# A two-layer network on one core: the last pair of heads by tiles, another rule for TensorE in the list planner, new due times, products of zeros

## The chip, the cores and the metric

The kernel runs on one core of a Trainium2 chip. The core has five engines with instruction queues of their own: PE (TensorE, the matmuls), DVE (VectorE), ACT (ScalarE), POOL (GpSimd) and SP (SyncE, which here only starts DMA transfers). Each engine works through its queue in order; waits between engines go through semaphores. The metric is the time of one execution on the device in microseconds, lower is better.

## The reference, cut to what matters

The input x has 4 sequences of 512 tokens with 512 features, in float32. Four blocks follow one another, each as x = x + layernorm(f(layernorm(x))).

```python
# 1: state space, 16 heads of 64 (1024 channels)
x = x + _layernorm(_L0_attn_ref(_layernorm(x), ...))
# 2: shared expert and 2 of 8 routed experts
x = x + _layernorm(_L0_ffn_ref(_layernorm(x), ...))
# 3: 16 heads of 128, a delta rule over time
def step(St, inp):
    q_, k_, v_, a_, b_ = inp
    sk = jnp.einsum('bhij,bhj->bhi', St, k_)
    err = sk - v_
    Sn = a_[..., None, None] * St - b_[..., None, None] * err[..., None] * k_[..., None, :]
    o_ = jnp.einsum('bhij,bhj->bhi', Sn, q_)
    return (Sn, o_)
...
o = (o - mu) * jax.lax.rsqrt(var + 1e-05) * ln_w + ln_b
g = jax.nn.sigmoid(x @ Wg).reshape(B, S, NH, D)
return (o * g).reshape(B, S, NH * D) @ Wo
# 4: 2 of 8 experts, chosen for a whole sequence
logits = x0 @ switch_w.T + switch_b
probs = jax.nn.softmax(logits, axis=-1)
gate, top_idx = jax.lax.top_k(probs, TOPK)
...
out = x + o
return out @ w3.T + b3
```

## The kernel before

Tokens are handled in tiles of 128 rows, four to a sequence (TPB). The program has three parts: `state_space` (block 1, up to some 430 us), `experts` (block 2, to some 900 us) and `upper_layer` (blocks 3 and 4, the rest).

**Opening.** SP first loads the first sequence's four tiles x[0] to x[3] (L266), then the identity matrix in `const` (L268), then in `state_space` the first half of w_in, the small parameters `prm`, half of w_gate, the other halves, the rest of `const`, and w_out (L380 to L386). POOL fills a tile `zero` (L395), which SP later writes over a buffer in memory (L474).

**Planned lists.** `state_space` and `upper_layer` don't issue their work directly. They describe it to a `Plan`: each `op` has an engine, a cost in us, a due time, the operations it comes after, and the buffers ("slots") it uses. `sequence` (L186) then simulates the engines by these costs: over and over, each engine's candidates are the operations whose predecessors are all placed, and the one that can start first is taken; among those that could start at the same time the earlier due time wins. `ahead` bounds how far past the earliest open due time an operation may be taken. The result is the fixed order of each engine's list; on the chip the semaphores decide when each instruction runs. For an operation of PE the model adds 0.2 us (`DRAIN`) before anything that comes after it may start, another PE operation included, and 0.1 us (`CROSS`) from engine to engine. A load in the model takes 0.42 us of SP and lands some 3.5 us later. Loads of x that start the first layer are a made-up engine "LD".

The due times are a sum of a sequence's or a pair's number and a parameter in `DUE` (L18). In the first layer the unit is a sequence: its norm is due at the number less `norm`, its projections at the number, the gate's at +`sigma`, the scans at +`scan`, the output products at +`out`. In the upper layer the unit is one of 32 pairs of heads (8 to a sequence).

**A sequence of the first layer** (`sequence(b, due)` within `state_space`): each x tile is loaded (L606), its mean and variance are taken on DVE (L434) and POOL, it is normalised into one of two `xn` buffers (L450), turned by four PE transposes (L618) and copied by ACT (L628). Projections (L462) take four products in one PSUM bank; ACT and three DVE instructions (L676) make a convolution of them, which frees the bank. The tag `mm` has four banks.

**A pair of heads**: `prepare` projects and convolves q, k, v, makes the masked score blocks and stores 32x32 blocks to memory; `solve` loads them back as `lb` (L1722), solves by rows on DVE (L1748, L1757), stores the result and loads it into `yi` (L1766, L1773); `merge` builds full inverses with small PE products and copies `xx`, `wt`, `w`, `yi` (L1795, L1807); `recur` goes through four chunks of 128 tokens in sequence; each chunk leaves a tile `o` for both heads and sums of squares `ss`. `finish` (L2028) waits for all chunks, computes 8 reciprocal roots at once on POOL, scales 8 pieces of `o` on ACT (L2071), turns four pieces per head (L2085), applies the norm's weights while moving to `oT` (L2092), multiplies the gate on POOL (L2106), and multiplies by `wo` for the four tiles (16 instructions), adding to `y` (L2148).

After a sequence's last pair `route` norms y, adds the row from memory (L2222), stores it back (L2231), norms it again in place (L1224, once the store has landed), turns it into `zT`, and computes the router's logits; DVE then chooses experts and mixes their weights. `experts_of` applies them (L2446, L2465) and ends with products by `w_o`, a norm, a sum (L2502) and the output's store (L2510). `begin` gathers the next sequence's rows and prepares its input.

The main loop at the end of `upper_layer` calls these for the 32 pairs.

Of the kernel before, what the change touches and what calls it, by code (L numbers as in the profile page):

```python
# [9 lines left out]
F32 = mybir.dt.float32  # L10
# [5 lines left out]
BANKS = {"mm": 4, "tr": 2, "sq": 2}  # L16

DUE = dict(  # L18
    half=0.13, last=0.17, out=1.7, norm=0.27, late=0.0, dt=0.28, sigma=0.66, scan=1.76, early=3.8,
    seam=0.18, head=0.5, qkv=0.1, score=0.0, keys=0.46, solve=0.83, rows=0.2, merge=1.73,  # L20
    recur=1.45, step=0.44, finish=2.42, gate=0.0, turn=0.07, sum=0.88, route=3.33, begin=0.77,
    spread=1.55, ahead=3.0, last_finish=2.86, last_route=2.65, last_spread=0.0, fetch=0.6,
    pick=0.03, experts=1.07, next=0.38, experts2=1.62, experts3=2.7, close3=0.36, tile=0.02,
    half_router=0.0, mix=0.68, close=0.15, closes=0.0,
)
ENGINES = [getattr(mybir.EngineType, n) for n in ("PE", "DVE", "Activation", "Pool", "SP")]

P = 128
# [80 lines left out]
class Plan:  # L109
# [59 lines left out]
    def sequence(self):  # L169
        for n, op in enumerate(self.ops):  # L170
            op.place = (op.due, n)
            op.missing = len(op.after)
            for o in op.after:
                o.then.append(op)
        waiting, clock, order = {}, {}, []
        self.held, table = {"DVE": 0.0, "POOL": 0.0}, None
        by_due = sorted(self.ops, key=lambda op: op.place)
        first = 0
        for op in self.ops:
            clock.setdefault(op.engine, 0.0)  # L180
            waiting.setdefault(op.engine, [])
            if not op.missing:
                waiting[op.engine].append(op)
        while len(order) < len(self.ops):
            while by_due[first].missing < 0:
                first += 1  # L186
            limit = by_due[first].due + self.ahead
            best = None
            for engine, ops in waiting.items():
                pick = None  # L190
                for op in ops:
                    if op.due > limit:
                        continue
                    at = self.start(op, clock[engine])
                    if at is not None and (pick is None or (at, op.place) < pick[:2]):
                        pick = (at, op.place, op)
                if pick and (best is None or pick[0] < best[0]):
                    best = pick
            assert best, "no operation can start"
            at, _, op = best  # L200
            waiting[op.engine].remove(op)
            for slot in op.slots:
                tag = self.tags[slot.tag]
                if slot not in tag["live"]:
# [46 lines left out]
def network(ctx: ExitStack, tc: tile.TileContext, a: dict, out: bass.AP):  # L251
# [6 lines left out]
    def ps(tag, shape=(P, 512)):  # L258
        return psum.tile(list(shape), F32, tag=tag, name=tag, bufs=BANKS[tag])
# [107 lines left out]
    def state_space():  # L367
        with (
# [768 lines left out]
    def upper_layer(first):  # L1137
        with (
# [41 lines left out]
            def row(shape=(P, D)):  # L1180
                return plan.slot(pl, "row", shape, ROWS, free=True)

            def lateslot(tag, shape, bufs):
                return plan.slot(plan.late, tag, shape, bufs)
# [840 lines left out]
                        )  # L2025
                return o, ss, outs, used

            def finish(seq, pair, o, ss, outs, y, due):  # L2028

                rs = lateslot("rso", [P, UNITS], 2)  # L2030

# [174 lines left out]
            def route(b, y, sums, due):  # L2206
# [2 lines left out]
                before = stored[b]  # L2209
                part = lateslot("part", [P, E2, KD], 1)  # L2210
                turned, prods, written = [], [], []
                for i in range(TPB):
# [26 lines left out]
                    turned.append(columns(zT, z, i, due + 0.1, [no]))  # L2239

# [279 lines left out]
            for n in range(B * NPAIR):  # L2520
                b, pair = divmod(n, NPAIR)
                if pair == 0:
# [12 lines left out]
                o, ss, outs, last = recur(heads, yi, inverse, n + DUE["recur"])  # L2535
                used[n] = [last, *inverse]
                sums = finish(
                    seq, pair, o, ss, outs, y, n + DUE["finish" if n < B * NPAIR - 1 else "last_finish"]
                )
                if pair == NPAIR - 1:  # L2540
                    routed.append(route(b, y, sums, n + DUE["route" if b < B - 1 else "last_route"]))
# [103 lines left out]
```

## Time and profile before

| | us |
|---|---|
| median of 3 runs | 2992.0 (2986.73 to 2998.78) |
| the profiled execution | 2973.44 |
| its span, first to last instruction | 2971.6 |
| PE busy | 2828.6 (95%) |
| DVE busy | 1831.5 (62%) |
| ACT busy | 1174.8 (40%) |
| POOL busy | 694.8 (23%) |
| mean granted clock of PE | 0.978 |

The span runs from the first to the last instruction; the profiled execution's time is 1.8 us longer than it. Busy shares are means over stages. The page also cuts the span into 40 slices of 74 us and gives each engine's busy share in tenths, 9 standing for 90% or more:

```profile
PE   8999999999998999899989899998999999999997
PEld 3444444455554456565645555554556655555553
DVE  4887532011114666776688776687786678867455
ACT  4653221111111355444544444453444544544530
POOL 1233403100004113321231422132231222221133
```

The first six slices are the first layer's state space, the next six its experts, and from the thirteenth on the pairs of heads follow. A timeline row has a start, a duration, the engine and line, the operation, output and input, the number of merged instructions, and in brackets how long the engine had been idle and what ended that.

### The profile page before, as it was taken

To read this page: it belongs to the slowest core of one execution; us is meant where nothing else is said; L and a number is where in the kernel's file an instruction comes from. 1 tells how busy PE (TensorE), PEld (TensorE's weight loads), DVE (VectorE), ACT (ScalarE), POOL (GpSimd) and SP (SyncE) were. 2 spreads that over 40 slices of the span, in tenths; PEclk is the share of its full clock that TensorE was granted. 3 is DMA by queue.
4 is the path that set the end of the run, shared out by engine and by line. 5 is a ranking of instruction groups with operands and counts; after the bars stand their busy time and mean duration, and the time that the engine had idled before them with its cause. 6 is when DMAs were issued, how large, how long until landed. Compare 5 with 4: busy or idle time off the path is not lost. (4 is left out here: it accounts for less than half of the span.)

```text
span 2971.6 us, 38915 instructions
## 1 busy us (share of the span) xinstructions
PE 2828.6 (95%) x13095; PEld 1579.5 (53%) x13095; DVE 1831.5 (62%) x4629; ACT 1174.8 (40%) x2423; POOL 694.8 (23%) x859
## 2 busy tenths in 40 slices
PE   8999999999998999899989899998999999999997
PEld 3444444455554456565645555554556655555553
DVE  4887532011114666776688776687786678867455
ACT  4653221111111355444544444453444544544530
POOL 1233403100004113321231422132231222221133
PEclk9999999999999999999999999998999999999999
DMA  5321213698983434433454433345432435533332
GB/s 190 95 87 41 89 46 129 220 320 316 318 280 108 124 77 104 123 83 85 100 140 144 134 89 92 84 129 158 123 116 70 97 98 139 140 82 81 100 128 89
DMA packets 289705, 383.99 MB, mean 129 GB/s; under 512 B 127490, under 2 KB 128130, under 8 KB 289250
## 3 DMA queue, kind: packets, MB, share of 16 engines
q1 hardware_dynamic: 275600, 347.51, 40.3%
q0 software_dynamic: 5120, 16.78, 1.6%
q10 hardware_dynamic: 8786, 17.22, 1.6%
q8 instruction: 104, 1.70, 0.2%
q14 instruction: 95, 0.78, 0.1%
HBM read 320.58 MB, written 60.82 MB: 128 GB/s over the span
## 5 line engine op out<-in xcount | busy, mean ns | idle before, releaser
L1199 PE MATMUL mm<-xT,wh 128*128 128x512 f32 x1536 | 739.1, 602 | 1.0 <-DVE cv L1590 1.0
L1590 DVE SCALAR_TENSOR_TENSOR cv<-mm,prm,cv 128x511 f32<-128x511 f32 (+2 forms) x576 | 427.2, 745 | 134.7 <-ACT cv L1579 124.8
L1199 PEld LDWEIGHTS mm<-xT,wh 128*128 128x128 f32 x1536 | 269.8, 192 | 218.4 <-issue 207.1
L1199 PE MATMUL mm<-wo,oT 128*128 128x512 f32 x512 | 271.4, 645 | 5.5 <-POOL oT L2106 1.8
L1748 DVE TENSOR_TENSOR term<-lb,xb 128x60 f32<-128x60 f32 (+24 forms) x992 | 213.2, 215 | 91.0 <-DMA lb<-blocks 75.5
L1199 PE MATMUL mm<-xT,wg 128*128 128x512 f32 x512 | 260.4, 596 | 0.1
L1757 DVE TENSOR_TENSOR xb<-xb,term 128x60 f32<-128x60 f32 (+24 forms) x992 | 226.7, 228 | 33.8
L1579 ACT ACTIVATE cv<-mm,prm 128x512 f32<-128x512 f32 x192 | 148.9, 776 | 192.5 <-PE mm L1199 189.3
L1672 POOL TENSOR_TENSOR kq<-qk,ag 128x384 f32<-128x384 f32 x128 | 119.3, 950 | 337.9 <-PE sq L1199 284.6
L1079 PE MATMUL mm<-gu,rT 128*128 128x352 f32 x624 | 190.9, 459 | 0.0
L1079 PEld LDWEIGHTS mm<-gu,rT 128*128 128x128 f32 x624 | 118.2, 190 | 76.1 <-issue 17.8
L1199 PE MATMUL sq<-S,kq 128*128 128x128 f32 x768 | 151.0, 279 | 6.8 <-DVE S L1963 6.8
L1199 PEld LDWEIGHTS sq<-S,kq 128*128 128x128 f32 x768 | 124.0, 193 | 44.0 <-issue 26.7
L1372 POOL DMA_INDIRECT got<-yg,index x32 | 37.6, 1174 | 446.1 <-DMA yg<-yo 365.7
L1199 PEld LDWEIGHTS mm<-wo,oT 128*128 128x128 f32 x512 | 94.0, 204 | 84.8 <-issue 67.9
L1605 ACT ACTIVATE qk<-cv 128x512 f32<-128x512 f32 x128 | 80.5, 629 | 136.6 <-DVE cv L1590 114.7
L1085 DVE TENSOR_TENSOR actr<-slr,mm 128x352 f32<-128x352 f32 x39 | 20.3, 521 | 183.1 <-PE mm L1079 178.6
L1199 PEld LDWEIGHTS sq<-const,vT 128*128 128x128 f32 x512 | 87.7, 192 | 80.2 <-issue 53.2
L462 PE MATMUL mm<-xT,w_in 128*128 128x512 f32 x256 | 123.2, 611 | 5.9 <-DVE cv L676 5.1
L1558 DVE TENSOR_TENSOR_SCAN m<-ag,m 128x516 f32<-128x516 f32 x64 | 95.7, 1499 | 52.2 <-DMA ag<-dd 38.2
L1199 PE MATMUL mm<-qk 128*128 128x256 f32 x512 | 123.7, 383 | 0.7 <-ACT qk L1605 0.7
L462 PE MATMUL mm<-xT,w_gate 128*128 128x512 f32 x256 | 123.3, 594 | 0.0
(302 smaller groups left out, 4778.2 us busy)
## 6 DMA issues: line engine op xcount, KB each, us to landing
gu<-in_gu SPq DMA_DIRECT2D x78, 704.0 KB
wh<-in_wh SPq DMA_DIRECT2D x192, 256.0 KB
ag<-dd SPq DMA_DIRECT2D x64, 516.0 KB
sw<-in_sw SPq DMA_DIRECT2D x96, 256.0 KB
dn<-in_dn SPq DMA_DIRECT2D x39, 512.0 KB
lb<-blocks SPq DMA_DIRECT2D x128, 128.0 KB
wg<-in_wg SPq DMA_DIRECT2D x64, 256.0 KB
wo<-in_wo SPq DMA_DIRECT2D x64, 256.0 KB
```

The source lines that it names most:

```text
L462: lambda: nc.tensor.matmul(p(), lhsT=lhsT(), rhs=rhs(), start=first, stop=last),
L1079: nc.tensor.matmul(dst, lhsT=rT[:, k, :], rhs=gu[:, k, lo : lo + F], start=k == 0, stop=k == KD - 1)
L1085: nc.vector.tensor_tensor(act, sl, pu, ALU.mult)
L1199: nc.tensor.matmul(dst, lhsT=lhsT, rhs=rhs, start=start, stop=stop)
L1372: nc.gpsimd.indirect_dma_start(out=to(), out_offset=None, in_=yg, in_offset=bass.IndirectOffsetOnAxis(ap=places[k][:, n : n + 1], axis=0), ...
L1558: nc.vector.tensor_tensor_scan(flat, ag()[:, 0, :], flat, 0.0, ALU.mult, ALU.add)
L1579: lambda p=p, cv=cv, j=j: nc.scalar.activation(cv(), p(), AF.Identity, bias=cb[:, j, h : h + 1], scale=cw[:, j, h, 3:4]),
L1590: lambda p=p, cv=cv, j=j, t=t: nc.vector.scalar_tensor_tensor(cv()[:, t:], p()[:, : S - t], cw[:, j, h, 3 - t : 4 - t], cv()[:, t:], ALU.mult,
L1605: lambda cv=cv, view=view: nc.scalar.activation(view(), cv(), AF.Silu),
L1672: lambda j=j: nc.gpsimd.tensor_tensor(kq()[:, j], chunk(qk()[:, j, :])[:, 1:, :], g()[:, 1:, j : j + P], ALU.mult,),
L1748: nc.vector.tensor_tensor(part(), lb()[:, i : i + 1, i + 1 :].to_broadcast([P, n, left]), xb()[:, :n, i : i + 1].to_broadcast([P, n, left] ...
L1757: nc.vector.tensor_tensor(rest, rest, part(), ALU.add)
```

## The change

It has these parts:

- In the planner, an operation of PE that comes after another one of PE may start when that one's cost is over; the 0.2 us of `DRAIN` are now added only towards other engines.
- 28 or so of the due parameters have other values, most of them in the first layer and in the last sequence's tail.
- `const`'s first part is loaded behind x[0] in place of x[3], and `prm` ahead of the weights.
- Six products of the zero tile into a bank of the tag `sq` stand at the head of PE's list.
- For the very last pair `finish` hands over to a new function `by_tile`: for each of the four tiles it scales, turns, moves, gates, multiplies by `wo` and adds to y, each tile coming after its own chunk's sums of squares.
- In `route` the second norm writes to y[i] instead of the row itself, so it no longer comes after the row's store; for the last sequence the tiles' due times step by `tile`.

```diff
@@ DUE
-    half=0.13, last=0.17, out=1.7, norm=0.27, late=0.0, dt=0.28, sigma=0.66, scan=1.76, early=3.8,
-    seam=0.18, head=0.5, qkv=0.1, score=0.0, keys=0.46, solve=0.83, rows=0.2, merge=1.73,
-    recur=1.45, step=0.44, finish=2.42, gate=0.0, turn=0.07, sum=0.88, route=3.33, begin=0.77,
-    spread=1.55, ahead=3.0, last_finish=2.86, last_route=2.65, last_spread=0.0, fetch=0.6,
-    pick=0.03, experts=1.07, next=0.38, experts2=1.62, experts3=2.7, close3=0.36, tile=0.02,
-    half_router=0.0, mix=0.68, close=0.15, closes=0.0,
+    half=0.12, last=0.43, out=2.02, norm=1.8, late=0.06, dt=0.0, sigma=0.87, scan=3.72, early=4.33,
+    seam=0.96, head=0.5, qkv=0.1, score=0.0, keys=0.46, solve=0.82, rows=0.29, merge=1.73,
+    recur=1.45, step=0.44, finish=2.42, gate=0.0, turn=0.07, sum=1.06, route=3.32, begin=0.98,
+    spread=1.55, ahead=3.0, last_finish=2.94, last_route=2.48, last_spread=0.27, fetch=0.53,
+    pick=0.46, experts=0.63, next=0.0, experts2=1.91, experts3=3.05, close3=0.17, tile=0.05,
+    half_router=0.0, mix=0.71, close=0.45, closes=0.0,
@@ Plan.sequence
             for o in op.then:
-                o.ready = max(o.ready, op.end + (self.CROSS if o.engine != op.engine else 0.0))
+                done = op.begin + op.us if o.engine == op.engine == "PE" else op.end
+                o.ready = max(o.ready, done + (self.CROSS if o.engine != op.engine else 0.0))
@@ network
+    const = glob.tile([P, CONST.shape[1]], F32, tag="const", name="const")
     for i in range(TPB):
         nc.sync.dma_start(x[i], x_in[i])
-    const = glob.tile([P, CONST.shape[1]], F32, tag="const", name="const")
-    nc.sync.dma_start(const[:, :P], a["const"][:, :P])
+        if i == 0:
+            nc.sync.dma_start(const[:, :P], a["const"][:, :P])
@@ state_space
+            nc.sync.dma_start(prm, a["p1"])
             for half in range(2):
...
-                    if w is w_in and not half:
-                        nc.sync.dma_start(prm, a["p1"])
...
+            idle = ps("sq")
+            for k in range(6):
+                nc.tensor.matmul(idle, lhsT=zero[:, :P], rhs=zero, start=True, stop=True)
...
-            for us, to in ((3.0, in_there), (0.6, None), (2.8, gate_there), (2.8, in_there), (2.8, gate_there)):
+            for us, to in ((0.6, None), (3.0, in_there), (2.8, gate_there), (2.8, in_there), (2.8, gate_there)):
@@ upper_layer
+            def by_tile(o, ss, rs, outs, gates, wos, y, due):
+                sums, oTs = [], [lateslot("oT", [P, S], 2) for _ in range(2)]
+                for i in range(TPB):
+                    d, two = due + DUE["tile"] * i, slice(2 * i, 2 * i + 2)
+                    def scale(two=two):
+                        rstd(rs()[:, two], ss()[:, two], EPS)
+                        nc.gpsimd.tensor_scalar(rs()[:, two], rs()[:, two], -(float(P) ** 0.5), None, ALU.mult)
+                    sc = op("POOL+", 1.2, d, scale, outs[two], [ss, rs])
...
+                    last = op("ACT", 0.6, d, scaled, [sc], [o[i], rs])
...
+                    last = op("PE", 0.35, d, turn, [last], [p, o[i], *oTs])
...
+                    last = op("ACT", 0.7, d, move, [last], [p, *oTs])
...
+                    last = op("POOL+", 0.75, d, gated, [last, *ready], [*oTs, *(g for g, _ in gates)])
+                    p = bank("mm")
+                    for j in range(2):
+                        wo, wl = wos[j]
+                        last = op("PE", 0.88, d, ..., [wl, last], [p, *oTs, wo, y[i]])
+                    sums.append(op("DVE", 0.7, d, ..., [last], [p, y[i]]))
+                return sums
...
-                sc = op("POOL+", 2.4, due, scale, outs, [ss, rs])
...
+                if last_pair:
+                    return by_tile(o, ss, rs, outs, gates, wos, y, due)
+                sc = op("POOL+", 2.4, due, scale, outs, [ss, rs])
@@ route
                 for i in range(TPB):
-                    xr = z = row()
+                    due = start + (DUE["tile"] * i if last else 0.0)
+                    xr, z = row(), y[i]
...
-                    no = normalised(z, xr, st, [xr], due, after=[written[i]])
+                    no = normalised(z, xr, st, [xr, z], due)
```

More of the change, by code (lines that the diff above doesn't have):

```diff
@@ L2026, in recur, with scaled, turn, move @@
                 return o, ss, outs, used
-            def finish(seq, pair, o, ss, outs, y, due):
+            def by_tile(o, ss, rs, outs, gates, wos, y, due):
[6 more added lines that the diff above has]
+                    sc = op("POOL+", 1.2, d, scale, outs[two], [ss, rs])
+                    def scaled(i=i):
+                        for j in range(2):
+                            nc.scalar.activation(
+                                o[i]()[:, j, :],
+                                o[i]()[:, j, :],
+                                AF.Copy,
+                                scale=rs()[:, 2 * i + j : 2 * i + j + 1],
+                            )
+                    last = op("ACT", 0.6, d, scaled, [sc], [o[i], rs])
+                    p = bank("tr")
+                    def turn(p=p, i=i):
+                        for j in range(2):
+                            nc.tensor.transpose(one(p(), j), o[i]()[:, j, :], ident)
+                    last = op("PE", 0.35, d, turn, [last], [p, o[i], *oTs])
+                    def move(p=p, i=i):
+                        for j in range(2):
+                            nc.scalar.activation(
+                                one(oTs[j](), i), one(p(), j), AF.Identity, bias=lnb, scale=lnw
+                            )
+                    last = op("ACT", 0.7, d, move, [last], [p, *oTs])
+                    def gated(i=i):
+                        for j in range(2):
+                            oT, gt = one(oTs[j](), i), one(gates[j][0](), i)
+                            nc.gpsimd.tensor_tensor(oT, oT, gt, ALU.mult)
+                    ready = [g for _, g in gates]
+                    last = op("POOL+", 0.75, d, gated, [last, *ready], [*oTs, *(g for g, _ in gates)])
+                    p = bank("mm")
+                    for j in range(2):
+                        wo, wl = wos[j]
+                        last = op(
+                            "PE",
+                            0.88,
+                            d,
+                            lambda i=i, j=j, p=p, wo=wo: mm(p(), one(oTs[j](), i), wo(), j == 0, j == 1),
+                            [wl, last],
+                            [p, *oTs, wo, y[i]],
+                        )
+                    sums.append(
+                        op(
+                            "DVE",
+                            0.7,
+                            d,
+                            lambda i=i, p=p: nc.vector.tensor_tensor(y[i](), y[i](), p(), ALU.add),
+                            [last],
+                            [p, y[i]],
+                        )
+                    )
+                return sums
@@ L2030, in finish @@
+            def finish(seq, pair, o, ss, outs, y, due, last_pair):
                 rs = lateslot("rso", [P, UNITS], 2)
@@ L2211, in route @@
                 turned, prods, written = [], [], []
+                last = b == B - 1
+                start = due
                 for i in range(TPB):
-                    xr = z = row()
+                    due = start + (DUE["tile"] * i if last else 0.0)
+                    xr, z = row(), y[i]
                     src = xs[b * TPB + i]
@@ L2237, in route @@
                     st = row_stats(xr, [xr], due, [ad])
-                    no = normalised(z, xr, st, [xr], due, after=[written[i]])
+                    no = normalised(z, xr, st, [xr, z], due)
                     turned.append(columns(zT, z, i, due + 0.1, [no]))
+                due = start
                 last = b == B - 1
@@ L2537, in upper_layer @@
                 sums = finish(
-                    seq, pair, o, ss, outs, y, n + DUE["finish" if n < B * NPAIR - 1 else "last_finish"]
+                    seq, pair, o, ss, outs, y, n + DUE["last_finish" if n == B * NPAIR - 1 else "finish"],
+                    n == B * NPAIR - 1,
                 )
```

## The prediction, made before the changed kernel was run

> **What bounds the kernel now.** I read the page's busy shares first, then PE's busy time by stage, PE's waits, the timeline of the first 45 us, that of the last 130 us, and last the stalls of the middle stage one by one. PE is busy 95% of the span, so only its idle time and its slow clock can be won.
>
> ```profile
> PE 2828.6 (95%) x13095; PEld 1579.5 (53%) x13095; DVE 1831.5 (62%) x4629; ACT 1174.8 (40%) x2423; POOL 694.8 (23%) x859
> ...
> 0.00:50.00 50.00, 36.62 (x85) 17.14 (x86) 21.81 (x40) 16.32 (x22) 6.64 (x20) 0.93 0.73 273
> 50.00:400.00 350.00, 349.58 (x912) 153.60 (x911) 248.48 (x455) 151.37 (x199) 112.76 (x112) 1.00 0.24 74
> ...
> 980.00:2800.00 1820.00, 1729.41 (x9708) 1035.58 (x9706) 1338.79 (x3670) 860.35 (x1916) 450.13 (x573) 0.97 0.42 109
> ...
> 2850.00:2900.00 50.00, 44.94 (x149) 24.98 (x150) 37.27 (x81) 8.62 (x14) 23.61 (x34) 0.97 0.44 153
> ...
> 2920.00:2940.00 20.00, 15.84 (x38) 5.67 (x38) 15.62 (x37) 3.81 (x5) 11.03 (x15) 0.95 0.31 105
> ```
>
> Each row gives a stretch, then PE's busy time first and the granted clock third from the end. PE idles 13.4 us in the first 50, 0.4 us in the rest of the first layer, 90.6 us in the 1820 us of the pairs of heads (where a mean clock of 0.97 costs another 45 to 64 us), and 5.1 and 4.2 us in two stretches of the tail. PE's waits name the causes:
>
> ```profile
> PE tr L1199 <- DVE xx L1795: 18.1, 9, 5.3
> PE tr L1199 <- ACT xx L1807: 15.6, 8, 5.9
> PE tr L1237 <- DVE row L1224: 13.0, 6, 6.3
> PE tr L1199 <- ACT w L1807: 11.8, 3, 5.4
> PE tr L1199 <- DVE kt L1701: 8.5, 4, 2.4
> PE tr L1199 <- issue: 7.6, 7, 3.4
> PE tr L618 <- DMA const<-in_const: 7.2, 1, 7.2
> ...
> PE mm L462 <- DVE cv L676: 5.1, 1, 5.1
> ```
>
> Total, times and longest wait follow each name. In 980 to 2800 there are 30 stalls of 0.8 us or more, 76.9 us together: 48.3 us in the merge of the inverses (xx, w and the unnamed ones), 28.6 us elsewhere. The worst merge stalls lie at the switches of sequences (1537 to 1670, 2009 to 2150, 2487 to 2613), where DVE waits up to 6 us for lb or yi to land.
>
> **Part A, the opening.** Removed: PE's first work waited for const at 7.17 although xn was there at 5.92; const now follows x[0]. Added: six products of zeros. A 128x512 f32 product is two instructions, 0.43 us each at full clock and 0.86 us at the opening's slow clock (weight loads follow at that distance from 13.20 to 15.76). With 4.2 us slow, as from 12.19 to 16.36, twelve take 5 x 0.86 + 7 x 0.43 = 7.3 us, from about 1.4 to 8.7; the third and fourth transposes wait for their norms (ending 9.3 and 10.3) anyway, so the projections would start near 11.6 instead of 12.19. Worth 0.6 us, and 2.1 us more if the clock then holds.
>
> The row on that: 16 transposes kept PE busy over 90% of 9.43 to 11.51 and the products behind them still ran at 0.86. The Trainium skill ("TensorE: Matmul & The Clock Gate", Part 4) says that transposes don't count as activity for the gate, and this row fits; by it the warmth would lapse again, and the 2.1 us be nothing.
>
> None of this reaches the end, because of the next wait:
>
> ```profile
> 12.19 9.91 PE L462 MATMUL mm<-xT,w_in 128*128 128x512 f32 x18 [0.67 <-ACT xT L628]
> ...
> 26.44 0.69 DVE L434 BATCH_NORM_STATS2 st<-x 128x6 f32<-128x512 f32 x1 [16.16 <-DMA x<-in_x]
> 28.35 0.55 DVE L450 TENSOR_SCALAR xn<-x,mv,rs 128x512 f32<-128x512 f32 x1 [0.20 <-POOL rs L439]
> ...
> 32.34 10.30 PE L462 MATMUL mm<-xT,w_in 128*128 128x512 f32 x18 [5.09 <-DVE cv L676]
> ```
>
> x[4], the second sequence's first tile, lands only at 26.44, behind 8 MB of weights, and DVE stands before it. The lists' model has it at 0.42 + 3.5 = 3.9. Before, its transpose was due at 1 - 0.27 = 0.73, behind the first half's projections (0 to 0.09), and ran at 43.8. Now norm=1.8 makes it due at -0.8. I followed the model's costs by hand: four tiles turned at 15.87, projections from 15.97, the transpose of x[4] ready at 18.2; the third product ends at 18.5 and the earlier due then wins. So PE does 6 instructions, then stands from 14 to 17 until the norm of x[4] ends at 28.9. After x[5]'s transpose (30.5) it lacks 26 of the 32 instructions that PE had done before at 27.25: 26 x 0.43 = 11.1, and some 1.5 for the slow clock, gives 43.1. Before reached the same point at 32.34 + 2.1 (clock) + 1.2 (the two transposes) = 35.6. Loss 7.5, I take **+8**; bounds -3 (the transpose stays where it was and the 2.7 us above count) and +15 (the whole wait, if the convolutions behind it fill the four banks again). The rest of this layer has 0.4 us to win; its new scan and out dues cost 0, with +10 as the worst, the 13.4 us of the opening being the nearest size of a badly placed list.
>
> **Part B, the last pair and its route.** Last squares end at 2843.4; then
>
> ```profile
> 2843.83 1.66 POOL L1203 TENSOR_TENSOR rso<-rso,mhalf 128x8 f32<-128x8 f32 x1
> ...
> 2849.66 2.52 POOL L2106 TENSOR_TENSOR oT<-oT,gt 128x512 f32<-128x512 f32 x2 [3.84 <-ACT oT L2092]
> ...
> 2850.99 7.13 PE L1199 MATMUL mm<-wo,oT 128*128 128x512 f32 x16 [1.78 <-POOL oT L2106]
> ...
> 2863.54 1.18 DVE L1224 TENSOR_SCALAR row<-row,mv,rs 128x512 f32<-128x512 f32 x1 [0.49 <-DMA xs<-row]
> ```
>
> and the last y at 2859.6: 16.2 us. By tile, the last one needs rstd 1.05 (0.22 + 0.57 + 0.22), two scalings 0.6, two transposes 0.3, two moves 0.6, two gatings 0.8 (between 2.52/4 and twice 1.26), two products 1.7, a sum 0.7, crossings 0.7: 6.5 us. The other three finish behind their chunks, 5.3 us apart. POOL issues 12 rstd instructions for 3 and 8 gatings for 2, ACT 8 moves for 2; POOL sat idle 29 us ahead of 2843, which hides them, and uncovered they cost about 4 us. Route writes z to y[i], so a norm no longer waits for the row's store to land (from the add's end at 2859.4 to 2863.5: some 2 us). The last zT copy (2877.9) can come about 18 us earlier. But PE has the same products to do, so the end gains at most PE's idle time between 2842 and 2940: 1.4 + 5.1 + 4.2, near 11. The 12 us behind PE's last product stay. I take **-8**, bounds 0 (the other dues of the tail open equal gaps) and -11.
>
> **Part C, no draining between TensorE operations.** The rows show no price for following one another: x18 products of w_in and the shared x18 (7.89 us) run at 0.43 to 0.44 an instruction, chained or alternated. What changes is order. With 0.2 us of drain in the model a chain's next product was never ready at once, so the lists alternated two chains: the two convolution inputs of the opening both started at 20.42, eight products after 12.19, where one alone takes 4 x 0.86. So a chain's result comes up to 3.4 us sooner. This shortens stalls that start in a projection or a sum, and moves the block stores of a pair forward, but not a DMA's landing. I take half of the 28.6 us and a quarter of the 48.3 us: **-26**. Bounds: -146 if all idle and slow clock went (no row speaks for that), more soberly -65; and +42 (below). The small dues (solve, rows, sum) are in this term.
>
> **Sum.** +8 - 8 - 26 = -26. The profiled execution took 2973.4 (span 2971.6 and 1.8 around it), so 2947 for such a run. The median of the three runs is 2992.0, 18.6 higher; against it 2966.
>
> **Rivals.**
> 1. The merge stalls go too. Earlier chains bring each pair's blocks to DMA earlier, and half of 76.9 us idle and half of 54 us clock go: 65 in place of 26, 2927. For it: stalls above 3 us are followed by 10 us windows at 0.67 to 0.83, so each counts nearly double. Against: these stalls end on lb and yi landing, which PE's order doesn't touch.
> 2. The middle gains nothing, since its stalls are DMA's, and the opening's loss eats the tail's gain: 2992.
> 3. Slower: begin=0.98 puts the next sequence's loads, gathers and norms 0.21 x 57 = 12 us earlier (57 is 1820 / 32 pairs), onto one more pair's block stores and lb loads in SP's queue. Price at one switch, by the pair of stalls at 1537 and 1552: 5.25 + 3.59 idle and 5.1 of clock (10 us windows at 0.75, 0.91, 0.83), 14 us; three switches 42: 3034. It decides from the second such switch, when it passes the middle's gain of 26. For it: SP waits 47 us for blocks to land and 742 for PE before loads already. Against: an earlier begin also takes its work off the crowded switch.
>
> **Chances.** Forecast 0.42 (its own range 2950 to 2984), rival one 0.12, two 0.19, three 0.27. A measurement here tells about 0.5%, 15 us, from no change. Faster by more: three quarters of the forecast's share, all of rival one, a little of rival two: 0.47. Within: 0.26. Slower: 0.27. The range 2930 to 3028 leaves out most of rival one's far side and half of rival three.
>
> **What would show it.** A: DVE's wait for x[4] still ending near 26.4, and a PE idle of 12 to 15 us before a transpose near 29; no such idle, and the hand-followed order was wrong. B: the last y sum some 9 us after the last squares or less, and PE idle under 3 us in the tail ahead of the last products. C: idle of PE in the pairs' stage at 60 to 70 us instead of 90, products of one bank in fours, first convolution inputs no longer in twos. If that idle is above 100 us and its stalls lie on lb or yi, rival three holds, and the forecast is wrong in C.

## The result and the profile after

Over 20 runs on each side the changed kernel has a median of 2982.85 us (2970.76 to 2992.72), the kernel before 2989.86 (2981.9 to 2998.78). The ratio is 0.9974, with a 95% interval of 0.9966 to 0.9982: about 8 us faster, a real difference, but inside the 0.5% that the prediction counts as no change. The forecast was 26 us.

The profiled execution of the changed kernel has a span of 2984.7 us, 13.1 more than that of before. 8.8 us of that is a single wait of PE in block 2, which the change doesn't touch (line L327 below). A second profile of the same kernel, taken beside the experiments and called `after_again`, doesn't have it: its experts' stage is 13.4 us shorter, and its span is 2963.2. To compare profiles I therefore cut each at the same events: the last w_out product of the first layer, the last gate and up product of the experts, the copy of `o` by which the first pair's recurrence ends, the same copy of the last pair, and the end. The differences between cuts, in us:

| | first layer | experts | to pair 0 | pairs | tail | span |
|---|---|---|---|---|---|---|
| before | 369.2 | 516.3 | 182.7 | 1774.4 | 129.1 | 2971.7 |
| after | 375.7 | 531.5 | 183.8 | 1771.9 | 121.8 | 2984.7 |
| after_again | 375.7 | 518.1 | 185.0 | 1764.0 | 120.4 | 2963.2 |

The first layer loses 6.5 us (forecast 8), the tail wins 7.3 to 8.7 (forecast 8), and the pairs win 2.5 to 10.4 (forecast 26). Four profiles with this same order of work in the pairs (these two, and the experiments `norm_back` and `x4_known` below) lie between 1763.0 and 1771.9, and two others with one order of work (`lb_known` and `both_known`) are 11 us apart, so single profiles differ by some 10 us there. The page's busy shares and the stretches of 0 to 50 and 980 to 2800 us, after the change:

```profile
PE 2829.7 (95%) x13107; PEld 1587.2 (53%) x13107; DVE 1828.2 (61%) x4629; ACT 1151.3 (39%) x2407; POOL 686.9 (23%) x874
```

```profile
0.00:50.00 50.00, 32.90 (x90) 15.99 (x90) 22.02 (x43) 13.13 (x20) 8.24 (x24) 0.86 0.75 273
980.00:2800.00 1820.00, 1728.63 (x9692) 1039.46 (x9691) 1341.52 (x3634) 829.61 (x1881) 453.87 (x582) 0.97 0.43 110
```

PE's busy time comes first after the stretch's length. In 980 to 2800 PE idles 1820 - 1728.6 = 91.4 us, where before it idled 90.6. Between the cuts of the pairs it idles 84.0 us (79.2 in after_again) where before it idled 88.0. The new rule for PE was to take 20 to 30 us off this. It hardly shrank; it changed its name. PE's waits after, total, times and longest:

```profile
PE sq L1204 <- ACT u L1941: 27.8, 15, 5.0
PE sq L1204 <- ACT yi L1812: 25.8, 6, 7.2
PE sq L1204 <- DVE S L1968: 17.9, 12, 4.3
PE tr L623 <- DVE xn L455: 15.4, 4, 13.6
PE mm L327 <- issue: 8.8, 1, 8.8
```

Before, the longest entries were the merge's xx and w (18.1, 15.6, 11.8, together 45.5); they are 3.3 us now. In their place stands the recurrence: its products wait for ACT's copies u and yi and for DVE's copy S, 71.5 us together, of which u and S had 8.8 before and yi none. None of these copies is a slow operation (0.4 to 0.6 us each), so ACT and DVE must be held up by something ahead in their queues. DVE's own wait for lb, first before the change, then after:

```profile
DVE term L1748 <- DMA lb<-blocks: 75.5, 24, 9.2
```

```profile
DVE term L1753 <- DMA lb<-blocks: 108.5, 29, 7.2
```

(lb is the tile of 32x32 blocks that DVE's row solving reads.) One stall shows how the two are linked, in the order of time (start, duration, engine, line; the brackets give the engine's idle time before the row and what ended it):

```profile
2557.34 0.87 SPq L1511 DMA_DIRECT2D sw<-in_sw  x2
2558.30 0.39 SPq L1511 DMA_DIRECT2D ag<-dd  x1
2558.85 0.35 SPq L1511 DMA_DIRECT2D wh<-in_wh  x1
2559.37 3.79 SPq L1727 DMA_DIRECT2D lb<-blocks  x4
```

```profile
2570.62 0.61 PE L1204 MATMUL sq<-r,yi 128*128 128x128 f32 x4
...
2571.06 0.19 DVE L1753 TENSOR_TENSOR term<-lb,xb 128x31 f32<-128x31 f32 x1 [6.07 <-DMA lb<-blocks]
...
2575.42 0.63 ACT L1610 ACTIVATE qk<-cv 128x512 f32<-128x512 f32 x1 [5.93 <-DVE term L1753]
...
2577.85 0.37 ACT L1941 COPY u<-sq 128x256 f32<-128x256 f32 x1
...
2578.27 0.93 PEld L1204 LDWEIGHTS sq<-u,kt 128*128 128x128 f32 x4 [5.29 <-ACT u L1941]
2578.27 1.22 PE L1204 MATMUL sq<-u,kt 128*128 128x128 f32 x4 [4.46 <-ACT u L1941]
```

The lists have DVE begin the next pair's row solving, and put a convolution behind it. DVE first uses lb 7.9 us after its last load was issued (2563.16 to 2571.06); it stands 6.07 us for it. ACT's next operation, qk, waits for that convolution, 5.93 us. ACT's copy of u stands behind qk, a table load and gt, though its product was done at 2571.2. PE stands 4.46 us for u. The planner takes lb to land 3.4 us after its issue, always. That one number of the model became the theory for the experiments.

### The profile page after: what moved, and what is told of

Same layout as the page of the kernel before. It is cut to its first block, busy times and chain, and to the rows that moved or that the text cites. A ratio compares the mean times of both kernels' runs of the same rounds, so it can differ in the third digit from the quotient of the medians.

```text
span 2984.7 us, 38935 instructions
## 1 busy us (share of the span) xinstructions
PE 2829.7 (95%) x13107; PEld 1587.2 (53%) x13107; DVE 1828.2 (61%) x4629; ACT 1151.3 (39%) x2407; POOL 686.9 (23%) x874
## 5 line engine op out<-in xcount | busy, mean ns | idle before, releaser
L1204 PE MATMUL mm<-xT,wh 128*128 128x512 f32 x1536 | 704.9, 598 | 0.0
L1204 PEld LDWEIGHTS mm<-xT,wh 128*128 128x128 f32 x1536 | 275.5, 191 | 263.0 <-issue 256.8
L1753 DVE TENSOR_TENSOR term<-lb,xb 128x60 f32<-128x60 f32 (+24 forms) x992 | 204.5, 206 | 125.2 <-DMA lb<-blocks 108.5
L1204 PE MATMUL mm<-wo,oT 128*128 128x512 f32 x512 | 256.8, 622 | 0.0
L1204 PE MATMUL mm<-xT,wg 128*128 128x512 f32 x512 | 251.7, 608 | 0.0
L1204 PE MATMUL sq<-S,kq 128*128 128x128 f32 x768 | 154.2, 283 | 23.0 <-DVE S L1968 17.9
L1204 PEld LDWEIGHTS sq<-S,kq 128*128 128x128 f32 x768 | 118.7, 195 | 28.0 <-DVE S L1968 20.4
L1090 DVE TENSOR_TENSOR actr<-slr,mm 128x352 f32<-128x352 f32 x39 | 20.3, 521 | 182.7 <-PE mm L1084 182.7
L1204 PEld LDWEIGHTS mm<-wo,oT 128*128 128x128 f32 x512 | 93.3, 202 | 71.4 <-issue 66.0
L1204 PEld LDWEIGHTS sq<-r,yi 128*128 128x128 f32 x512 | 80.2, 201 | 91.2 <-ACT yi L1812 33.0
L327 PE MATMUL mm<-xT,sgu 128*128 128x512 f32 x264 | 118.1, 603 | 10.9 <-issue 8.8
L1204 PE MATMUL mm<-qk 128*128 128x256 f32 x512 | 119.6, 386 | 6.8 <-ACT qk L1610 6.7
L1204 PEld LDWEIGHTS mm<-xT,wg 128*128 128x128 f32 x512 | 89.0, 193 | 66.4 <-issue 61.2
L467 PE MATMUL mm<-xT,w_in 128*128 128x512 f32 x256 | 115.3, 596 | 0.7 <-ACT xT L633 0.7
```

The lines of the kernel that those rows point to most:

```text
L327: nc.tensor.matmul(dst, lhsT=w(k), rhs=xT[:, k, :], start=k == 0, stop=k == n - 1)
L467: lambda: nc.tensor.matmul(p(), lhsT=lhsT(), rhs=rhs(), start=first, stop=last),
L1090: nc.vector.tensor_tensor(act, sl, pu, ALU.mult)
L1204: nc.tensor.matmul(dst, lhsT=lhsT, rhs=rhs, start=start, stop=stop)
L1753: nc.vector.tensor_tensor(part(), lb()[:, i : i + 1, i + 1 :].to_broadcast([P, n, left]), xb()[:, :n, i : i + 1].to_broadcast([P, n, left] ...
```

## The experiments

Each run was made beside the kernel before on the same chip, whose median was 2971.5 to 2974.6 there (15 to 18 us below that of the result's runs, so ratios are what to compare). A ratio below is to that kernel, with its 95% interval. Stages are those of the table above, from one profile each. Differences between whole runs are of medians where nothing else is said.

### The parts taken apart

**rule_alone**: the kernel before, with only PE's rule in `sequence`.

```diff
-                o.ready = max(o.ready, op.end + (self.CROSS if o.engine != op.engine else 0.0))
+                done = op.begin + op.us if o.engine == op.engine == "PE" else op.end
+                o.ready = max(o.ready, done + (self.CROSS if o.engine != op.engine else 0.0))
```

> The kernel before with only the planner's rule changed (a TensorE operation may follow another one of TensorE without the 0.2 us). Theory: the middle's idle time is set by when DVE gets lb and yi from DMA, so the rule only moves the stalls; time 0 +- 5 us against before, TensorE idle in the pairs' stage 85 to 95 us, no wait of 13 us in the opening (the old due times are kept). Rival 1 (the prediction's part C): 20 to 26 us faster, idle 60 to 70 us. Rival 2: the rule needs the new due times; alone it is 10 us or more slower.

Ratio 1.0021 (1.0001 to 1.0040): 5 us slower, not faster. Pairs 1777.4, which can't be told from before's 1774.4; tail 134.5, first layer 368.6. PE's longest entry is again the copy of u (36.2 us), and DVE's wait for lb is 112.0 us instead of 75.5:

```profile
DVE term L1749 <- DMA lb<-blocks: 112.0, 32, 10.8
```

**rule_out**: the changed kernel, with that edit undone.

> The changed kernel with the old rule of the planner (all its other parts kept). Theory: as the changed kernel within 5 us, that is 3 to 12 us faster than before. Rival 1: the rule is worth 20 to 26 us and the other due times lose it, so this is 10 to 20 us slower than before. Rival 2: the due times were worth it and the rule costs: 15 us or more faster than before.

Ratio 0.9943 (0.9922 to 0.9964), better than the whole change (0.9964 in after_again below; the intervals overlap a little, the stages don't). Pairs 1738.3, 36 us less than before; first layer 380.6, tail 132.8. DVE waits 52.7 us for lb. So the gain of the change in the pairs sits in the due times that I had called small, and the rule takes most of it away there, while the first layer and the tail are shorter with it.

**tail_alone**: the kernel before, with `by_tile`, the new `route` and the due times of the tail.

> The kernel before with the last pair by tiles, the route's second norm into y, and the due times of the tail alone. Theory: the stretch from the last chunk's copy of o to the end goes from 129 to about 122 us, 7 us faster than before; the rest is unchanged. Rival: the tail's gain in the changed kernel came from the rule and its other lists; here the tail stays at 127 to 131 us, time 0 +- 3 us.

Ratio 1.0021 (1.0003 to 1.0038), tail 134.9: 5.8 us longer, where 7 shorter were expected. Finishing by tiles alone doesn't shorten the tail.

**norm_back**: the changed kernel with `norm=0.27`.

> The changed kernel with norm=0.27 in place of 1.8. Theory: TensorE's 13.6 us wait before the transpose of x[4] goes, a wait of about 6 us for a free bank comes in its place some 14 us later, and the first layer ends 6 to 7 us sooner than in the changed kernel: 13 to 15 us faster than before. Rival: the early norms of the later sequences are worth something that pays for it, so the time is that of the changed kernel within 3 us.

Ratio 0.9967 (0.9952 to 0.9982); the first layer ends at 373.8, 1.9 us earlier than after (lb_known below, with the same first layer as after, ends it at 374.3, so at most part of this is the due time's). A miss: the wait of 13.6 us did go, and one of 6.56 us came in its place at 26.50, behind 32 product instructions, as expected; but the layer still ends 4.6 us later than before. PE goes on at 33.06 where before it did at 32.34, and then waits 1.18 and 1.08 us in front of products that before had no such wait. Where the other 1.6 us are was not found.

### The landing times

**after_again**: the changed kernel once more, as a measure for this chip.

> The changed kernel itself, for a second profile and on the chip of the three runs beside it. All theories: 0.3% faster than before (5 to 11 us); the experts' stage of the second block (from the first shared product to the last routed one) takes 516 us as in before's profile, not the 532 of the first profile of the changed kernel, whose TensorE once waited 8.8 us for its own instructions there; TensorE's 13.6 us wait for the transpose of x[4] is there again.

Ratio 0.9964 (0.9951 to 0.9977).

**lb_known**: the changed kernel, with the load of lb planned to land after 6.5 us. No instruction is added or removed, only the order of the lists follows.

```diff
-                    "SP", 1.75, due, take, [hd["given"] for hd in heads], [lb, blocks], landing=3.4
+                    "SP", 1.75, due, take, [hd["given"] for hd in heads], [lb, blocks], landing=6.5
```

> The changed kernel, with the planner told that lb lands 6.5 us after its issue in place of 3.4 (the traces show 5 to 8 us from the last issue to the first use where DVE stood waiting). Theory: the new rule costs because its lists bring DVE to the rows' solving before lb has landed (DVE waited 108 us for lb, 53 us with the old rule), ACT stands behind DVE and TensorE behind ACT; with the landing known DVE's wait for lb falls below 60 us and the time by 10 us or more against the changed kernel (15 us or more faster than before). Rival: the rule costs by another way, such as TensorE's long runs of one bank; DVE's wait falls but the time stays within 4 us of the changed kernel.

Ratio 0.9861 (0.9840 to 0.9882): 45 us below before and 36 below the change, or 41 and 31 by the ratios. The pairs take 1730.7. Stretch, DVE's wait, and PE's waits in this kernel:

```profile
980.00:2800.00 1820.00, 1757.17 (x10005) 1054.31 (x10005) 1361.11 (x3695) 896.26 (x1989) 451.42 (x588) 0.99 0.43 111
```

```profile
DVE term L1753 <- DMA lb<-blocks: 28.2, 15, 5.9
```

```profile
PE tr L1204 <- DVE xx L1800: 15.3, 12, 2.9
...
PE sq L1204 <- ACT yi L1812: 11.8, 5, 4.1
...
PE sq L1204 <- ACT u L1941: 6.0, 14, 0.6
PE sq L1204 <- DVE S L1968: 4.8, 5, 3.5
```

DVE's wait falls from 108.5 to 28.2 us. PE's idle time falls from 91.4 to 62.8 and the granted clock rises from 0.97 to 0.99. The three entries that had grown with the change, 71.5 us together, are 22.6; the longest is now the merge's xx, 15.3.

**x4_known**: the changed kernel, with the loads of the second sequence's x planned to land late, as they do.

```diff
-                            landing=3.5,
+                            landing=3.5 if b > 1 else 25.0,
```

> The changed kernel, with the planner told that the second sequence's x lands 25 us after its issue in place of 3.5. Theory: DVE takes the first convolution ahead of x[4], TensorE does 16 products ahead of its transpose, its 13.6 us wait shrinks to 3 us or less and the first layer ends 9 to 12 us sooner: 15 to 19 us faster than before. Rival: the four banks and ACT hold TensorE up instead, and the first layer ends less than 3 us sooner.

Ratio 0.9927 (0.9906 to 0.9948), 12 us below the change. The first layer ends at 368.0, 7.7 earlier (9 to 12 expected). 32 product instructions now run ahead of the second sequence's transposes, and PE's wait in front of them is 3.8 us where it was 13.6:

```profile
PE tr L623 <- DVE xn L455: 6.5, 3, 3.8
```

**rule_tail**: the changed kernel, with the new rule only for operations due from 32.5 on, which is the last pair's end and the tail.

```diff
+                follows = o.engine == op.engine == "PE" and o.due >= self.follow
-                done = op.begin + op.us if o.engine == op.engine == "PE" else op.end
+                done = op.begin + op.us if follows else op.end
```

> The changed kernel with the new rule only for operations due at 32.5 or later in the upper layer, which is from the last pair's recurrence on; the old rule everywhere else. Theory: the middle of the run without the rule (36 us shorter than before's from the first to the last pair's end) and the tail of the run with it (122 us after the last chunk, not 129 or 133): 25 to 31 us faster than before. Rival: the tail's gain is from the lists that lead to it, not from the rule there; the tail stays at 129 us or more and the time at that of the run with the old rule, 17 us faster than before, within 4 us.

Ratio 0.9912 (0.9891 to 0.9933). The pairs are those of rule_out (1738.2), the tail is that of the change (122.3 against rule_out's 132.8). The tail's gain needs both edits, the tiles and the rule: alone each leaves it longer than before's 129.1 (134.9 in tail_alone, 134.5 in rule_alone).

### Together, and on the kernel before

**both_known**: lb at 6.5 and x at 25 in the changed kernel.

> The changed kernel with both landings told to the planner: lb 6.5 us after its issue, the second sequence's x 25 us. Theory: the two gains lie in different stages and add: 41 and 12 us less the changed kernel's own 8 counted once, that is 48 to 56 us faster than before. Rival: the first layer's end only moves the later stages against DMA in another way and part is given back; 35 to 43 us faster.

Ratio 0.9854 (0.9829 to 0.9879), no better than lb_known: the 6.2 us won in the first layer (368.1) come back as a longer stage of pairs (1741.9 against 1730.7). PE, DVE and ACT work through the pairs in the same order in both traces, so the lists are not the reason; whether the 11 us are chance, or come from when the stage starts, is open.

**lb_known_rule_out**: lb at 6.5, old rule.

> The changed kernel with lb's landing of 6.5 us told to the planner and the old rule for TensorE. Theory: with the landing known the new rule is right in itself, as the prediction's part C had it, so this is 10 to 25 us slower than the same with the new rule: 16 to 31 us faster than before. Rival: the rule is worth nothing in either case, and the landing alone makes the gain: 37 to 45 us faster than before.

Ratio 0.9887 (0.9863 to 0.9911). Pairs 1728.0 against 1730.7 with the new rule, tail 133.1 against 121.7, first layer 380.0 against 374.3. With lb's landing known, the rule costs the pairs nothing that can be told and wins them nothing, where 10 to 25 us were expected; what it wins lies in the tail and the first layer. DVE waits 13.8 us for lb here.

**lb_known_before**: the kernel before with lb at 6.5, the one number alone.

> The kernel before with nothing changed but lb's landing in the planner, 6.5 us in place of 3.4. Theory: DVE's wait for lb falls from 75 to below 40 us and with it the merge's stalls; 8 to 25 us faster than before. Rival: with the old rule DVE comes late to lb anyway, so the lists only shift; within 5 us of before.

Ratio 0.9862 (0.9840 to 0.9885), as good as lb_known, and more than the 8 to 25 us expected. Pairs 1737.9, DVE's wait for lb 27.8.

**lb_later**: both_known with lb at 8.5.

> As the run with both landings told to the planner, but lb's at 8.5 us in place of 6.5. Theory (DVE's wait for lb sets it): the wait falls from 29 to under 15 us, and the time by 0 to 10 us against 6.5, 43 to 53 us faster than before, since little is left to win there. Rival: the landing is now later than the real one, the solving starts late, and the pairs' stage grows by 10 us or more: at most 33 us faster than before.

Ratio 0.9950 (0.9934 to 0.9965). DVE now waits only 12.5 us for lb, but the pairs take 1756.9:

```profile
980.00:2800.00 1820.00, 1745.79 (x9809) 1050.14 (x9807) 1358.41 (x3680) 840.78 (x1920) 453.11 (x577) 0.98 0.42 110
```

PE idles 74.2 us where lb_known has 62.8. DVE now comes to lb a median of 8.2 us after its last issue, when the last packet of lb has mostly been in for some time (median 3.7 us), and other stalls grow: that the late solving makes them is the likely reason, and was not isolated. A short wait alone is no sign of a short stage: lb_known_rule_out has about the same wait and the shortest pairs.

### Which due time

Three kernels take the changed one with the old rule (rule_out) and set one due time back.

**begin_back**: `begin=0.77`.

> The changed kernel with the old rule, as in the run without the rule, and begin=0.77 in place of 0.98. The run without the rule took 36 us less than before between the first and the last pair, which must come from the due times of this stage. Theory: the earlier begin is the larger part of it, so 10 us or more of that is lost here (3 to 9 us faster than before). Rival (the prediction's third): an earlier begin costs, so this is 5 us or more faster than the run without the rule (22 us or more faster than before). If neither, the other due times (sum, rows, solve) made it and this stays at 13 to 21 us faster.

Ratio 0.9923 (0.9898 to 0.9947) against rule_out's 0.9943; pairs 1732.9. The intervals overlap.

**rows_back**: `rows=0.2`.

> The changed kernel with the old rule and rows=0.2 in place of 0.29. If the later due times of the solving's rows made it, the pairs' stage takes 1755 us or more and the kernel is at most 8 us faster than before; if not, 1728 to 1745 us and 13 to 23 us faster.

Ratio 0.9933 (0.9915 to 0.9951), pairs 1736.0: no effect that can be told.

**sum_back**: `sum=0.88`.

> The changed kernel with the old rule, as in the run without the rule, and sum=0.88 in place of 1.06. If the later due time of the products by wo is what shortened the pairs' stage (1738 us without the rule against 1774 before), the stage takes 1755 us or more here and the kernel is at most 8 us faster than before. If it is not, the stage stays at 1728 to 1745 us, 13 to 23 us faster than before.

Ratio 1.0028 (1.0013 to 1.0043), pairs 1762.7. This one brings 24 of the 36 us back. The wait for lb, in rule_out and in sum_back:

```profile
DVE term L1752 <- DMA lb<-blocks: 52.7, 20, 8.1
```

```profile
DVE term L1752 <- DMA lb<-blocks: 76.7, 24, 8.0
```

With `sum` at 0.88 it is near the 75.5 us of before again. `sum` is when a pair's products with wo and DVE's additions to y are due. DVE doesn't come later to lb with the later `sum` (a median of 1.8 us after its last issue in rule_out, 2.2 in sum_back); lb is in sooner, with a median of 1.6 us from the last issue to its last packet against 2.5. That the due acts only through this wait was not isolated.

## Why the prediction went as it did

**Part A held for the wait for x[4], in mechanism and nearly in size; its small gain at the start didn't come.** The timeline of the opening:

```profile
1.34 7.57 PE L400 MATMUL sq<-zero 128*128 128x512 f32 x12 [1.34 <-POOL zero L396]
```

```profile
13.16 2.84 PE L467 MATMUL mm<-xT,w_in 128*128 128x512 f32 x6 [0.68 <-ACT xT L633]
...
27.14 0.69 DVE L439 BATCH_NORM_STATS2 st<-x 128x6 f32<-128x512 f32 x1 [15.42 <-DMA x<-in_x]
...
29.64 2.11 PE L623 MATMUL tr<-const,xn 128*128 128x128 f32 x8 [13.63 <-DVE xn L455]
```

Six product instructions, then 13.63 us of nothing before the second sequence's transposes at 29.64; predicted were six, 12 to 15 us, and near 29. The zeros took 7.57 us (7.3 predicted). But the projections start at 13.16, not near 11.6, and so later than the 12.19 of before: with const loaded ahead of it x[1] comes later (its statistics start at 5.71, 4.30 before), and the third and fourth norms, taken as unmoved, end at 10.72 and 11.72. (The 16 transposes that the prediction puts in 9.43 to 11.51 ran from 7.17 on.) The long wait covers this loss. The first layer ends 6.5 us later (8 predicted). x4_known takes 7.7 us off, so it is this late landing, unknown to the planner, that costs; norm_back, which only moves the due time, takes at most 1.9, so the blame that I gave to `norm` itself holds for a small part. The zeros were not tried by themselves.

**Part B held in size, not in its working.** The tail is 7.3 us shorter in the profiles on record. But PE idles 7.7 us from 2850 to 2940, where under 3 were to be left, and the last y sum was to come within 9 us of the last squares, and here it ends 13.8 us behind them:

```profile
2863.61 0.19 ACT L2021 ACTIVATION_READ_ACCUMULATOR squares<-o 128x1 f32 x1
...
2870.56 1.05 POOL L2074 TENSOR_TENSOR oT<-oT,gt 128x128 f32<-128x128 f32 x2
...
2871.00 3.70 PE L1204 MATMUL tr<-w4o,qk 128*128 128x512 f32 x8
...
2874.97 1.88 PE L1204 MATMUL mm<-wo,oT 128*128 128x512 f32 x4
...
2876.89 0.69 DVE L2094 TENSOR_TENSOR y<-y,mm 128x512 f32<-128x512 f32 x1 [0.42 <-PE mm L1204]
```

The last tile is gated at 2871.6, 7.8 us behind the squares, where the forecast's steps up to there make 3.4 us and the crossings: the engines had other work in between, which the forecast had left out. Its product runs at 2874.97 only, behind eight product instructions with w4o (L1204 at 2871.00). That costs nothing, since PE is not idle there. From the last copy of `o` to the end, before and after:

```profile
2842.50:2971.60 129.10, 106.12 (x314) 49.09 (x310) 76.55 (x177) 22.10 (x41) 52.97 (x73) 0.95 0.36 122
```

```profile
2862.90:2984.70 121.80, 101.63 (x296) 47.15 (x294) 74.30 (x174) 18.08 (x33) 50.31 (x74) 0.92 0.37 128
```

PE is busy 101.6 of 121.8 us where it was 106.1 of 129.1. So 4.5 of the 7.3 us are PE work that now lies ahead of the last pair's end, and 2.8 are less idle time. And the tiles alone do none of it (tail_alone 134.9, rule_out 132.8); only with the rule does the tail shrink (rule_tail 122.3). The prediction had given the rule no part in it.

**Part C failed, and it is the step that made the forecast wrong.** "This shortens stalls that start in a projection or a sum ... I take half of the 28.6 us and a quarter of the 48.3 us: -26." The pairs won 2.5 us in the profile on record, 10.4 in the second, and PE's idle time in them stayed at 91. The prediction saw that the stalls ended on lb and yi landing, and that a DMA's landing would not move, and still let an earlier chain shorten them. The merge's entries did shrink, from 45.5 to 3.3 us, but the recurrence's grew by more than that.

What the step missed is that the landing does move: the rule's lists let lb land later. Counted in the traces over the 32 pairs, where lb's packets can be told by their 4096 bytes, in us from SP's last issue of a pair's lb:

| | last packet of lb ends, median | pairs of 32 in which it ends after 3.4 | DVE comes to lb, median | DVE's wait for lb, total |
|---|---|---|---|---|
| before | 2.1 | 11 | 2.2 | 75.5 |
| rule_alone | 5.1 | 22 | 2.8 | 112.0 |
| after | 5.0 | 25 | 2.8 | 108.5 |
| rule_out | 1.6 | 3 | 1.8 | 52.7 |
| lb_known | 4.2 | 20 | 5.3 | 28.2 |

So DVE doesn't come to lb any sooner after its issue under the rule; it stands longer because lb is later, and what the lists have put behind DVE's instruction, on ACT and then on PE, stands with it. The rule is the only difference between the first two rows, and between the next two. In the 2 us ahead of a pair's first lb load SP had issued a mean of 0.28 MB of other large transfers before, 0.51 in rule_alone and after, and 0.12 in rule_out, which fits a queue in which lb stands behind more; that alone was not tried. lb_known doesn't undo this, it plans for it: DVE comes 2.5 us later, its wait falls to a quarter, and the kernel is 31 to 36 us below the change. With lb planned so, the rule costs the pairs nothing (lb_known_rule_out). The small due times, booked in the same term at no value of their own, were worth 36 us under the old rule, 24 of them `sum`'s.

**The rivals.** Rival one, merge stalls gone as well, did occur in part (xx and w left the list), but the idle time went to the recurrence, so its price didn't. Rival two, a middle that gains nothing while the opening's loss eats the tail's gain, is nearest to what happened, with 2992 against a median of 2982.9 and the forecast's 2966; its reason, that the middle's stalls are DMA's, is right as far as it goes. Rival three, an earlier `begin` that costs 14 us a switch, isn't seen: begin_back, with the later begin, is 5.4 us of pairs faster than rule_out, which is its direction but with overlapping ratios, where 42 were priced.

**The best kernels.** lb_known (0.9861), both_known (0.9854) and lb_known_before (0.9862) can't be told apart; each is about 1.4% faster than the kernel before, four to five times what the change gives. The last needs one number of the planner and none of the change.

## What to carry to other kernels

Where a list is planned from a model of costs, compare the model's landing times with the trace for every load that an in-order engine waits on: an engine that stands for a load doesn't wait alone, it holds what others need. A landing is no constant of the load: another order of work moved lb's by 3 us, and a model with a fixed landing can't see that, so a rule that looks more right can still give a list that is no faster. And less waiting is not the goal by itself: at 8.5 us DVE waited least and the kernel lost two thirds of both_known's gain.

## What the runs showed of the hardware

**The landing of lb.** In the stall shown, 256 x 2 + 516 + 256 KB (sw, ag, wh) were issued within 2 us ahead of lb's four transfers of 128 KB each, all on one queue, and from 2557 to 2572 the DMA engines were 81% busy at 179 GB/s. lb's own packets moved from 2562.5 to 2569.5. 1.28 MB ahead and 0.51 MB of its own take some 10 us at that rate, an estimate; from 2557.34 the last of lb was used at 2571.06, 13.7 us later. The Trainium skill ("DMA: Bandwidth & Descriptors", "Anatomy of one DMA — SWDGE (gpsimd) path") gives a fit for a single transfer made from another queue, 2 us and the bytes by 436 GB/s; for 0.51 MB that is 3.2 us, an estimate close to the 3.4 of the planner. This stall doesn't agree; that what lies ahead in the queue makes the difference fits the estimate of 10 us, but was not tried by itself. Of the planned values tried (3.4, 6.5, 8.5) the runs put 6.5 first.

**The clock after the zeros.** The profile shows a granted clock of 1.00 in these first stretches in both kernels, so here half speed is read from the products themselves, an instruction every 0.86 us instead of 0.43. Before the change 16 transposes from 7.17 to 11.51, with 0.3 and 0.7 us of idle between and behind them, didn't bring full speed: the products behind them ran at half speed from 12.19 for another 4.2 us. After it the zeros had brought it by 5.7, the eight transposes at 8.75 took 1.04 us instead of 1.94, and the products from 13.16 ran at full speed, though only the 16 transposes had run in the 4.3 us since the zeros' end. The granted clock fell to half at 19.36, 3.4 us into the wait for x[4], and was full again at 33.0. The Trainium skill ("TensorE: Matmul & The Clock Gate", Part 4) says that the full clock doesn't engage for transposes, which don't count as busy in the same way; the opening before fits that. If they counted for nothing at all, the clock should have fallen in the 4.3 us of transposes here, longer than the 3.4 us of idle after which it fell later, and it held. No run tried this by itself.

**One stall without a cause in the profile.** PE waited 8.8 us for nothing that the profile shows, in the profile on record, at the start of a product of the experts; in the second profile of the same kernel it isn't there.
